# An adaLN megakernel: feed-forward's inner units in single PSUM banks, and empty places between the variance and its root's use

## The chip, the cores and the metric

The kernel runs on one core of a Trainium2 chip, as one launch. The metric is the time on the device in microseconds (us). A core has five queues of instructions that run side by side and wait for each other by semaphores: TensorE (PE, matrix products, with its weight loads shown as PEld), VectorE (DVE), ScalarE (ACT, functions by table), GpSimd (POOL) and SyncE (SP, which starts the DMAs). Matrix products land in PSUM, eight banks of 128 partitions by 512 numbers[...].

## The reference, cut to what matters

The input is 2 sequences of 2048 tokens with 128 features. There are two blocks, each of this form, where the six vectors of each block come from a small modulation:

```
h = layernorm(x) * (1 + ca) + sa ;  x = x + ga * attention(h)
h = layernorm(x) * (1 + cb) + sb ;  x = x + gb * ffn(h)
```

In the first block the attention is a chunked delta-rule form, and its "ffn" is a whole local transformer of six layers with 16 heads and a window of 32. In the second block the attention is a linear-attention layer with its own two layer norms and a Gelu feed-forward, and its "ffn" is a local transformer of two layers with 8 heads and a window of 64. A layer of a local transformer is

```
x = x + local_attention(shift(x) @ Wqkv) @ Wo     # l2-normed, scaled, rotary q and k; softmax
t = shift(x);  v = mean((t - mean(t))**2)
n = (t - mean(t)) / sqrt(v + 1e-5) * g + b
a, gate = split(n @ W1 + b1)                      # 341 units each
x = x + (a * gelu(gate)) @ W2 + b2
```

The norm thus goes variance, root, use of the root. Everything is computed in float32.

## The kernel before, in words

After the first attention (up to about 570 us of the profile) the function `local_models` does the rest: eight layers, six with 16 heads and two with 8. Each layer is 32 tiles of 128 tokens (16 of each sequence, the sequences in turn), 256 tiles in all, and one loop at its end runs over them. In round `i` of that loop the tiles are at different stages: scores of tile i+1, projection of tile i+3 (`project`, L871 to L904), output of tile i.

*A round on PE, in order:* scores (`ps_s`, L986 masks and L995), the first projection (`ps_qk`, L871), the transposes of the softmax's weights (`ps_pT`, L1030), the second projection (only with 16 heads), weights times values (`ps_o`, L1047), values of tile i+2 (`ps_v`, L955), transposes of the output (`ps_oT`, L1063) and of q and k (`ps_turn`, L936), the output projection (`ps_y`, L1075).

*What DVE does in a round:* maximum and shift of the scores (L1003, L1005), two rotary products `r` and `t` for each projection (L881, L886), the row sums of the weights (L1019), the sums of squares (L897), a fast inverse root in eight small instructions that ends in `rq_y` (L167 to L180), and the residual `hs` (L1081). POOL adds r and t (L892), multiplies by the root (L904) and normalises the weights (L1021). ACT squares (L873), takes Exp (L1012) and copies nearly all that leaves PSUM.

*PSUM:* two pairs of banks (`wide`, pool `f_psA`) and four single banks (`bank`, pool `f_psT`). Scores and projections take the pairs in turn. A pair that held a projection comes free when `rq_y` is done, since the root's scratch lies in it.

*Feed-forward.* When four tiles of a sequence are done, `feed_forward` puts six steps for the 512 tokens on a list, and a round takes two places of the list, one after its first projection and one before `project_out`. The steps: `centre` (PE L1103, squares on ACT L1105), `variance` (DVE L1112 and L1115, and the power -0.5 on POOL, L1117), `scale` (PE turns the root into rows, `ps_r` L1135; DVE multiplies, L1138), `gate` and `up` (each through `hidden`, three matmuls L1156; Gelu on ACT L1166, product on DVE L1173) and `down` (PE L1181, sums on DVE L1187). Two sequences give two such blocks in eight tiles.

*Linear attention of the second block.* It works on 512 tokens at a time too. Its 27 steps (the tuple returned by `linear`) are on a second list, of which a round takes six places. They begin when the sixth layer's feed-forward of these tokens is done, and run beside the tiles of the sixth and the seventh layer, about 3520 to 4440 us of the profile. The steps hold three norms: before a3 and f3 `variance` also scales the centred rows on POOL (`xc`, L1120) and the next step turns them on PE (`normed`, `ps_n` L1128); before d4 the root itself is turned (L1135). A place with `rest` is a step that does nothing. A loop at the head of layer seven would take steps until the tokens it needs are ready.

*What sets the order.* The text of the loop gives each engine's order to a list scheduler of the framework, which may move an instruction ahead of others in its engine's queue, and it names the banks when it does so. So the order of the built program has to be looked at, not only the text.

The lines of the loop that take the steps:

```
lstep()                                    # before scores, before and after the rest of project ...
step()                                     # after the first projection
...
step()                                     # after the turns, before project_out
```

Of the kernel before, what the change touches and what calls it, by code (L numbers as in the profile page):

```python
# [24 lines left out]
HSZ = (128, 128, 85)  # L25
# [47 lines left out]
def tile_kernel(ctx: ExitStack, tc: tile.TileContext, a: dict, out: bass.AP):  # L73
# [27 lines left out]
    def bc(ap, shape):  # L101
        return ap.to_broadcast(list(shape))
# [605 lines left out]
    def local_models(mA, mB, hs0):  # L708
# [3 lines left out]
        wk = ctx2.enter_context(tc.tile_pool(name="f_k", bufs=1))  # L712
        lw = ctx2.enter_context(tc.tile_pool(name="l_w", bufs=1))
# [3 lines left out]
        def wide(name):  # L717

            return psA.tile([128, 1024], F32, tag="A", name=f"ps_{name}")

        def bank(name):
            return psT.tile([128, 512], F32, tag="T", name=f"ps_{name}")
# [366 lines left out]
        def step():  # L1089
            if steps:  # L1090
                steps.pop(0)()

        def lstep():
            if lsteps:
                lsteps.pop(0)()
# [3 lines left out]
        def centre(S, x, pool, keep):  # L1099
            p = bank("c")  # L1100
            for j in range(4):
                js = slice(j * 128, (j + 1) * 128)
                nc.tensor.matmul(p[:, js], lhsT=x[:, js], rhs=cen, start=True, stop=True)  # L1103
            S["sq"] = pool.tile([128, 512], F32, name="fsq")
            nc.scalar.activation(S["sq"], p, AF.Square)  # L1105
            if keep:
                S["xc"] = pool.tile([128, 512], F32, tag="t1", name="xc")
                nc.scalar.copy(S["xc"], p)

        def variance(S, pool):  # L1110
            ve = pool.tile([128, 4], F32, name="fve")
            nc.vector.tensor_reduce(  # L1112
                ve, S.pop("sq").rearrange("p (j d) -> p j d", j=4), AX.X, ALU.add
            )
            nc.vector.tensor_scalar(ve, ve, 1.0 / 128.0, 1e-5, ALU.mult, ALU.add)  # L1115
            rt = S["rt"] = pool.tile([128, 4], F32, name="frt")
            nc.gpsimd.tensor_tensor(rt, ve, bc(nhalf, (128, 4)), ALU.pow)  # L1117
            if "xc" in S:
                v = S["xc"].rearrange("p (j d) -> p j d", j=4)
                nc.gpsimd.tensor_tensor(v, v, bc(rt.unsqueeze(2), (128, 4, 128)), ALU.mult)  # L1120
# [10 lines left out]
        def scaled(S, x, out):  # L1131
            p = bank("r")
            rt = S.pop("rt")
            for j in range(4):
                nc.tensor.transpose(  # L1135
                    p[:, j * 128:(j + 1) * 128], bc(rt[:, j:j + 1], (128, 128)), ident
                )
            nc.vector.tensor_tensor(out, x, p, ALU.mult)  # L1138


        def feed_forward(g, b, blk):
            m, l = layers[g]
            n0 = blk * 512
            x = hs[1][:, b, n0:n0 + 512]
            S = {}

            def scale():
                S["x"] = wk.tile([128, 512], F32, tag="fsq", name="fx")
                scaled(S, x, S["x"])

            def hidden(base):
                pw = wide("f")
                ps_ = [pw[:, 0:512], pw[:, 512:1024], bank("f")]
                for c, sz in enumerate(HSZ):
                    o = base + 128 * c
                    nc.tensor.matmul(  # L1156
                        ps_[c][0:sz], lhsT=wts[g, "w1"][:, o:o + sz], rhs=S["x"],
                        start=True, stop=True,
                    )
                return ps_  # L1160

            def gate():
                for c, p in enumerate(hidden(HID)):
                    sz = HSZ[c]
                    u = S[c] = wk.tile([128, 512], F32, name=f"u{c}")
                    nc.scalar.activation(  # L1166
                        u[0:sz], p[0:sz], AF.Gelu, bias=wts[g, "c"][0:sz, 3 + c:4 + c]
                    )

            def up():  # L1170
                for c, p in enumerate(hidden(0)):
                    sz = HSZ[c]
                    nc.vector.scalar_tensor_tensor(  # L1173
                        S[c][0:sz], p[0:sz], wts[g, "c"][0:sz, c:c + 1], S[c][0:sz],
                        ALU.add, ALU.mult,
                    )

            def down():
                p = bank("fy")
                for c, sz in enumerate(HSZ):  # L1180
                    nc.tensor.matmul(  # L1181
                        p, lhsT=wts[g, "w2"][0:sz, c, :], rhs=S[c][0:sz],
                        start=(c == 0), stop=(c == 2),
                    )
                for lo, sh in ((0, 0), (64, 1)):
                    cs = slice(n0 + sh, n0 + sh + 512)
                    nc.vector.scalar_tensor_tensor(  # L1187
                        hs[0][lo:lo + 64, b, cs], p[lo:lo + 64, :], m.vec[lo:lo + 64, l, 8:9],
                        hs[1][lo:lo + 64, b, cs], ALU.add, ALU.add,
                    )  # L1190
                if l == m.depth - 1:
                    lsteps.extend((linear if m is models[0] else output)(b, blk))

            steps.extend((
                lambda: centre(S, x, wk, False), lambda: variance(S, wk), scale, gate, up, down,
            ))

        def outer(b, k, gate, x):
# [55 lines left out]
        def linear(b, k):  # L1254
            S = {}
# [8 lines left out]
            def a0():  # L1264
                outer(b, k, mA, S["x"])

            def rest():
                pass

            def a3():  # L1270
                p = normed(S)
# [139 lines left out]
            def f3():  # L1411
# [8 lines left out]
                ready.add((b, k))  # L1420

            return (
                fetch, rest, a0, lambda: centre(S, S["x"], lw, True), lambda: variance(S, lw), a3,
                rest, lambda: centre(S, S["h"], lw, False), b2, b3, b4, rest, c1, c2, c3, c4, d1,
                rest, lambda: centre(S, S["x1"], lw, False), lambda: variance(S, lw), d4, e1, e2,
                rest, lambda: centre(S, S.pop("x"), lw, True), lambda: variance(S, lw), f3,
            )


# [37 lines left out]
        for i in range(-3, n):  # L1467
            j = i + 3
            lstep()
            if 0 <= i + 1 < n:  # L1470
                scores(i + 1)
# [3 lines left out]
            if j < n:  # L1475
                g, b, t = tiles[j]
                jj = j % per
                nu = len(layers[g][0].units)
                more = g < last
                if g == second and t % 4 == 0:  # L1480
                    while (b, t // 4) not in ready:
                        lstep()
                if nu == 2:
                    project(j, 0)
                if more and jj == 4:
                    load_proj(g + 1, 0)
                if more and jj == 6 and g + 1 == second:
                    models[1].consts()
                if jj == 6 and g == second - 1:
                    linear_consts()  # L1490
                if more and jj == 8:
                    factors(g + 1)
                    if 2 == 2:
                        load_out(g + 1)
                if more and jj == 18:
                    load_ff(g + 1)
                if more and jj == 22:
                    fold_ff(g + 1)
                if nu == 2 and more and jj == per - 1:
                    load_proj(g + 1, 1)  # L1500
                lstep()
# [27 lines left out]
            if i >= 0:  # L1529
                g, b, t = tiles[i]  # L1530
                project_out(i)
                if 2 == 1 and i % per == per - 1 and g < last:
                    load_out(g + 1)
                if t % 4 == 3:
                    feed_forward(g, b, t // 4)
# [9 lines left out]
    with ExitStack() as ctx2:  # L1545
        local_models(m0, m1, hs0)
# [63 lines left out]
```

## Time and profile before

Three runs took 5069.89, 5073.97 and 5086.58 us.

| | |
|---|---|
| median of the runs | 5073.97 us |
| the profiled execution's own time | 5073.89 us |
| its span, first to last instruction | 5072.1 us |
| mean granted PE clock | 0.959 |
| PE busy | 4591.6 us, 91% |
| DVE busy | 3984.3 us, 79% |
| ACT busy | 2861.4 us, 56% |
| POOL busy | 2781.8 us, 55% |
| HBM traffic | 10 GB/s |

The span lies within 1.8 us of the profiled execution's time. The busy time of an engine counts its own instructions, not the time in which its queue stood at a semaphore; the list of waits gives the latter, by the instruction that waited and by what released it. A line like "PE ps_qk L871 <- DVE rq_y L180: 52.6, 51, 3.1" says that the matmul at line 871 waited 51 times for the instruction at line 180, 52.6 us in all and 3.1 at the longest.

### The profile page before, as it was taken

The page shows a single profiled execution, that of the slowest core. Times are in us where ns is not written, and L with a number is a line of the kernel's source. Part 1 is how long each engine was busy: PE and PEld are TensorE (multiplying, and loading weights), DVE is VectorE, ACT ScalarE, POOL GpSimd, SP SyncE. Part 2 cuts the span into 40 slices and gives each one's busy share as a digit, 9 for nine tenths or more (in the row PEclk, how much of TensorE's full clock was granted, in tenths as well). Part 3 has the DMA queues.
Part 4 walks back from the last instruction along what each step waited for, and adds up shares of the span by engine and source line. Part 5 has one row for each costly group of instructions (what it writes and reads, how often), then busy time and mean ns, then how long its engine had stood idle before and what let it go on. Part 6 is the DMA issues. An engine that isn't in the chain of part 4 may idle for free.

```text
span 5072.1 us, 170859 instructions
## 1 busy us (share of the span) xinstructions
PE 4591.6 (91%) x74850; PEld 3154.3 (62%) x74850; DVE 3984.3 (79%) x6840; ACT 2861.4 (56%) x4645; POOL 2781.8 (55%) x1666
## 2 busy tenths in 40 slices
PE   5667799999999999999999999999989898899887
PEld 4445566666666666666666666666666565566554
DVE  6993488888887888788888888888776776688886
ACT  3323356666666666566666666666555554565554
POOL 3332366666665666566666666666555443355553
PEclk8777899999999999999999999999999999999999
DMA  2000222223222322222222222232122211111111
GB/s 76 1 1 24 83 70 63 63 72 79 63 66 63 81 67 71 60 76 69 63 67 66 77 70 67 63 78 68 48 54 52 53 45 40 36 45 43 54 52 41
DMA packets 222489, 295.61 MB, mean 58 GB/s; under 512 B 75656, under 2 KB 95408, under 8 KB 221744
## 3 DMA queue, kind: packets, MB, share of 16 engines
q1 hardware_dynamic: 221744, 284.67, 21.6%
q8 instruction: 591, 9.68, 0.8%
q14 instruction: 154, 1.26, 0.1%
HBM read 40.98 MB, written 10.75 MB: 10 GB/s over the span
## 4 chain that ended last, share of the span: by engine, by line
PE 52%; DVE 21%; ACT 7%; POOL 6%; issue 3%; DMA 1%; POOLq 0%; DVEq 0%; SPq 0%; ACTq 0%
PE ps_qk L871 12%; PE ps_turn L936 5%; PE ps_y L1075 5%; PE ps_v L955 5%; PE ps_o L1047 4%; PE ps_f L1156 4%; DVE t L886 4%; DVE ps_qk L897 4%; POOL r L892 4%; PE ps_s L995 4%; PE ps_fy L1181 3%; PE ps_oT L1063 3%; ACT sq L873 3%; DVE r L881 3%; DVE rs L1019 2%
## 5 line engine op out<-in xcount | busy, mean ns | idle before, releaser
L892 POOL TENSOR_TENSOR r<-r,t 128x1024 f32<-128x1024 f32 x448 | 1061.0, 2368 | 1034.1 <-DVE t L886 940.8
L873 ACT ACTIVATE sq<-ps_qk 128x1024 f32<-128x1024 f32 x448 | 460.1, 1027 | 1093.2 <-PE ps_qk L871 1085.9
L904 POOL TENSOR_TENSOR r<-r,rq_y 128x1024 f32<-128x1024 f32 x448 | 845.8, 1906 | 418.6 <-DVE rq_y L180 416.3
L871 PE MATMUL ps_qk<-wp,hs 128*128 128x512 f32 x1792 | 891.1, 620 | 88.2 <-DVE rq_y L180 63.6
L886 DVE TENSOR_TENSOR t<-ps_qk,tb 128x1024 f32<-128x1024 f32 (+1 forms) x512 | 553.2, 1080 | 173.3 <-POOL r L892 173.3
L1021 POOL TENSOR_TENSOR sm<-sm,rs 128x1024 f32<-128x1024 f32 x256 | 488.3, 1908 | 291.1 <-DVE rs L1020 207.3
L881 DVE TENSOR_TENSOR r<-ps_qk,tb 128x1024 f32<-128x1024 f32 (+1 forms) x512 | 548.7, 1072 | 113.2 <-ACT sq L873 108.7
L897 DVE TENSOR_REDUCE ps_qk<-sq 128x16 f32<-128x1024 f32 x448 | 548.5, 1224 | 10.7
L1047 PEld LDWEIGHTS ps_o<-v,pT 64*32 64x32 f32 (+1 forms) x26624 | 357.9, 108 | 281.9 <-ACT pT L1031 158.3
L871 PEld LDWEIGHTS ps_qk<-wp,hs 128*128 128x128 f32 x1792 | 308.3, 192 | 351.1 <-issue 236.6
L1047 PE MATMUL ps_o<-v,pT 64*32 64x64 f32 (+1 forms) x26624 | 422.9, 223 | 58.5 <-ACT pT L1031 32.4
L1075 PEld LDWEIGHTS ps_y<-oT,wo 128*128 128x128 f32 x3584 | 432.3, 193 | 62.7 <-issue 55.2
L955 PE MATMUL ps_v<-wp,hs 128*128 128x512 f32 x896 | 461.7, 631 | 1.0 <-issue 1.0
L936 PE MATMUL ps_turn<-ident,r 128*128 128x128 f32 x3584 | 448.3, 278 | 7.3 <-POOL r L904 5.8
L1075 PE MATMUL ps_y<-oT,wo 128*128 128x128 f32 x3584 | 447.1, 277 | 1.9 <-ACT oT L1064 1.9
L936 PEld LDWEIGHTS ps_turn<-ident,r 128*128 128x128 f32 x3584 | 411.5, 144 | 13.4 <-POOL r L904 10.6
L1003 DVE TENSOR_REDUCE mx<-ps_s 128x16 f32<-128x1024 f32 (+1 forms) x256 | 313.1, 1223 | 122.4 <-PE ps_s L995 118.9
L1156 PE MATMUL ps_f<-fx,w 128*128 128x512 f32 (+1 forms) x768 | 370.4, 606 | 6.1 <-DVE z L1290 3.5
L995 PE MATMUL ps_s<-kT,qT 64*32 64x64 f32 (+1 forms) x26624 | 366.5, 229 | 0.6 <-issue 0.6
L995 PEld LDWEIGHTS ps_s<-kT,qT 64*32 64x32 f32 (+1 forms) x26624 | 317.3, 107 | 62.1 <-issue 46.1
L1031 ACT COPY pT<-ps_pT 128x512 f32<-128x512 f32 x512 | 273.8, 585 | 143.3 <-PE ps_pT L1030 143.0
L1019 DVE TENSOR_REDUCE rs<-sm 128x16 f32<-128x1024 f32 (+1 forms) x256 | 310.0, 1211 | 53.9 <-ACT sm L1012 53.2
(267 smaller groups left out, 7555.9 us busy)
## 6 DMA issues: line engine op xcount, KB each, us to landing
v<-vn SPq DMA_DIRECT2D x1276, 128.0 KB
v<-vn SPq DMA_DIRECT2D x744, 64.0 KB
v<-vn SPq DMA_DIRECT2D x64, 256.0 KB
wp<-in_L_ffn_Wqkv SPq DMA_DIRECT2D x20, 512.0 KB
xD<-xb SPq DMA_DIRECT2D x24, 256.0 KB
xb<-xD SPq DMA_DIRECT2D x24, 256.0 KB
cs<-in_cos SPq DMA_DIRECT2D x128, 32.0 KB
cs<-in_sin SPq DMA_DIRECT2D x128, 32.0 KB
```

What stands on the lines that cost most here:

```text
L871: nc.tensor.matmul(pq[:, js], lhsT=hw, rhs=wts[g, u][:, js], start=True, stop=True)
L873: nc.scalar.activation(sq, pq, AF.Square)
L881: nc.vector.tensor_tensor(r[:, es].rearrange("p (h d) -> p h d", d=DH), pq[:, es].rearrange("p (h d) -> p h d", d=DH), bc(tb[:, 0, s].unsq ...
L886: nc.vector.tensor_tensor(t2[:, es].rearrange("p (h s d) -> p h s d", s=2, d=32), pq[:, es].rearrange("p (h s d) -> p h s d", s=2, d=32)[: ...
L892: nc.gpsimd.tensor_tensor(r, r, t2, ALU.add)
L897: nc.vector.tensor_reduce(pq[:, 16 * v:16 * v + 16], st[i].pop(("sq", v)).rearrange("p (h d) -> p h d", d=DH), AX.X, ALU.add,)
L904: nc.gpsimd.tensor_tensor(rv, rv, bc(y[:, 16 * v:16 * v + 16].unsqueeze(2), (128, 16, DH)), ALU.mult)
L936: nc.tensor.transpose(p[:, c * 128:(c + 1) * 128], r[:, cs], ident)
L955: nc.tensor.matmul(p, lhsT=hw, rhs=wv, start=True, stop=True)
L995: nc.tensor.matmul(sp[W * w:W * w + W, c0:c0 + 2 * W], lhsT=qT[64 * q:64 * q + 64, cc, W * w:W * w + W], rhs=kT[64 * q:64 * q + 64, cc, W ...
L1047: nc.tensor.matmul(po[s][W * w:W * w + W, co:co + 64], lhsT=pT[kp, q, c, W * w:W * w + W], rhs=v2[kp, w, co:co + 64], start=True, stop=True,)
L1075: nc.tensor.matmul(py[:, 0:128], lhsT=wts[g, "o"][:, c * NO + s, :], rhs=oT[:, s, c, :], start=(c + s == 0), stop=(c == 3 and s == NO - 1),)
```

## The change

Three edits. `hidden`, which serves gate and up, takes three single banks in place of a pair and one single bank. `rest`, the empty step, is defined for all. And an empty step is put between `variance` and the step that uses its result: once in the feed-forward's list (six steps become seven), and three times in the linear attention's (27 become 30). Line numbers after the first edit shift by three, and by two from `hidden` on.

```diff
+        def rest():
+            pass
+
@@
             def hidden(base):
-                pw = wide("f")
-                ps_ = [pw[:, 0:512], pw[:, 512:1024], bank("f")]
+                ps_ = [bank("f") for _ in HSZ]
                 for c, sz in enumerate(HSZ):
@@
             steps.extend((
-                lambda: centre(S, x, wk, False), lambda: variance(S, wk), scale, gate, up, down,
+                lambda: centre(S, x, wk, False), lambda: variance(S, wk), rest, scale, gate, up,
+                down,
             ))
@@
-                fetch, rest, a0, lambda: centre(S, S["x"], lw, True), lambda: variance(S, lw), a3,
+                fetch, rest, a0, lambda: centre(S, S["x"], lw, True), lambda: variance(S, lw), rest,
+                a3,
                 rest, lambda: centre(S, S["h"], lw, False), b2, b3, b4, rest, c1, c2, c3, c4, d1,
-                rest, lambda: centre(S, S["x1"], lw, False), lambda: variance(S, lw), d4, e1, e2,
-                rest, lambda: centre(S, S.pop("x"), lw, True), lambda: variance(S, lw), f3,
+                rest, lambda: centre(S, S["x1"], lw, False), lambda: variance(S, lw), rest,
+                d4, e1, e2,
+                rest, lambda: centre(S, S.pop("x"), lw, True), lambda: variance(S, lw), rest,
+                f3,
```

More of the change, by code (lines that the diff above doesn't have):

```diff
@@ L1265, in a0 @@
                 outer(b, k, mA, S["x"])
-            def rest():
-                pass
             def a3():
```

## The prediction

> **What bounds the kernel now.** I read the page first: TensorE (PE) is busy 91% of the span, and most of the chain that ended last is PE.
>
> ```profile
> PE 4591.6 (91%) x74850; PEld 3154.3 (62%) x74850; DVE 3984.3 (79%) x6840; ACT 2861.4 (56%) x4645; POOL 2781.8 (55%) x1666
> ...
> PE 52%; DVE 21%; ACT 7%; POOL 6%; issue 3%; DMA 1%; POOLq 0%; DVEq 0%; SPq 0%; ACTq 0%
> ```
>
> Next, the busy times tile by tile, cut where `project_out` (L1075) starts, for eight tiles of the six 16-head layers. Columns: start and end, length, busy time of each engine.
>
> ```profile
> 1852.54:1868.00 15.46, 15.28 (x328) 11.42 (x327) 13.65 (x23) 10.20 (x19) 11.74 (x8) 1.00 0.31 77
> 1868.00:1886.51 18.51, 17.43 (x330) 12.03 (x329) 16.72 (x27) 12.30 (x21) 13.05 (x8) 1.00 0.33 82
> 1886.51:1907.47 20.96, 19.93 (x331) 12.67 (x330) 16.39 (x32) 13.34 (x21) 12.22 (x9) 1.00 0.20 52
> 1907.47:1922.50 15.03, 15.03 (x327) 11.30 (x326) 11.57 (x14) 8.53 (x15) 7.44 (x5) 1.00 0.21 50
> 1922.50:1941.13 18.63, 17.46 (x331) 12.05 (x330) 16.84 (x27) 12.31 (x21) 13.95 (x9) 1.00 0.35 88
> 1941.13:1961.32 20.19, 19.70 (x331) 12.57 (x330) 16.39 (x32) 13.24 (x21) 11.46 (x8) 1.00 0.18 45
> 1961.32:1975.73 14.41, 14.36 (x320) 10.33 (x318) 10.90 (x13) 7.94 (x14) 7.59 (x4) 1.00 0.25 59
> 1975.73:1990.74 15.01, 14.37 (x321) 10.31 (x320) 13.16 (x22) 9.77 (x18) 10.45 (x7) 1.00 0.29 74
> sum 138.20, PE 133.58 PEld 92.69 DVE 115.61 ACT 87.61 POOL 87.91; mean PE 16.70 PEld 11.59 DVE 14.45 ACT 10.95 POOL 10.99
> ```
>
> Rows 1 to 3 carry one feed-forward block (centre and variance; scale and gate; up and down), rows 4 to 6 another, rows 7 and 8 none. PE is idle 138.20-133.58 = 4.6 us in eight tiles: all that any reordering can win here, 20 such groups giving 92 us. What ends PE's waits, by stage (first the 16-head layers, 900 to 3500 us; then 3520 to 4440, where the linear attention of the second block runs beside the tiles; then the last 630 us):
>
> ```profile
> PE ps_qk L871 <- DVE rq_y L180: 52.6, 51, 3.1
> PE ps_o L1047 <- ACT pT L1031: 18.0, 38, 0.5
> ```
> ```profile
> PE ps_n L1128 <- POOL xc L1120: 47.3, 14, 7.2
> PE ps_r L1135 <- POOL frt L1117: 18.6, 5, 5.1
> ```
> ```profile
> PE ps_oT L1063 <- ACT on L1053: 16.3, 25, 0.9
> PE ps_o L1047 <- ACT pT L1031: 10.2, 29, 1.2
> ...
> PE ps_r L1135 <- POOL frt L1117: 6.8, 4, 4.3
> ```
>
> The middle pair is PE standing behind the root and the scaling on POOL in the linear attention's norms: 66 us. In the feed-forward of the 16-head layers the same root waits for PE, not PE for it, as the timeline shows (root at 1506, used at 1512.6):
>
> ```profile
> 1506.08 1.03 POOL L1117 TENSOR_TENSOR frt<-fve,nhalf 128x4 f32<-128x4 f32 x1
> ...
> 1512.63 0.60 PE L1135 MATMUL ps_r<-ident,frt 128*128 128x128 f32 x4
> ```
>
> ScalarE's table switches, one to Gelu and one back to Exp for nearly each of 64 feed-forward blocks:
>
> ```profile
> L1012 ACT ACT_TABLE_LOAD x68 | 87.2, 1283 | 19.0 <-DVE sm L1005 17.9
> L1166 ACT ACT_TABLE_LOAD x62 | 79.5, 1283 | 0.5
> ```
>
> **What the Trainium skill says.** "TensorE: Matmul & The Clock Gate" (section Architectural detail) has matmuls in order with only weight loads pulled ahead, and ACT and DVE strictly first in, first out: the waits above, with everything behind them late, agree. "PSUM — Partial Sum Buffer" (PSUM bank collisions) wants PSUM guarded by bank, so a bank is free only when its last reader is done; here that makes qk wait for rq_y, 52.6 us. "Perfetto Trace Analysis" (Optimization Strategy) reads a gap that repeats on the saturated engine as perhaps too few PSUM buffers; the repeating 0.5 us behind pT and 1 us behind rq_y fit. "ScalarE: Activation LUTs" (What ACT_TABLE_LOAD costs) prices a switch at 1283 ns and a drain of 1380 ns; the trace agrees on 1283, and shows no drain (load at 1523.35, Gelu at 1524.64).
>
> **The change, part by part.** No arithmetic, DMA or operand is added or removed; SP's queue keeps its entries. Three things move; the built order of both programs shows how.
>
> *Single banks.* Gate and up no longer take two of the four banks that scores and qk alternate in; they take three of the other four. The wait this removes, qk behind a Gelu, is not in the list of waits: worth 0 by itself. New waits: behind up, the second pT, v and o now stand on the u products (DVE). Beside L1075-to-L1047 work of 7 us these products, the first ahead of r0, are done 1 to 2 us before: 0.
>
> *The empty place in the feed-forward.* Two places per tile, six steps become seven, so the two blocks of a group now fall differently. The order of a group becomes: root transposes; gate and up; down and centre; nothing; root and gate; up and down; nothing; centre. Removed: the split up (one of its matmuls among the pT transposes), with 18.0/18.6 groups = 0.97 us of pT waits per group (900 to 3500 us holds 18.6 groups of 139.7 us). Left: one tile where three Gelus and a table load stand on ACT between Exp and the pT copies. Worked from durations: qk starts at 0, ends 1.95; scores' shift on DVE done 3.1, Exp (1.06) 4.15, load 5.45, three Gelus (about 0.65) 7.5, pT copy 8.1; PE has by then done gate (2.6), pT, the second qk and two mask matmuls, 7.7: waits 0.45. Saved 0.5.
> The qk wait: in a light tile DVE's loop is about 15.0 us against 14.4 of PE (rows 7, 8); the variance adds 0.87 to DVE, the root's product 0.68, a centre 0.6 to PE (15.03-14.41), root transposes 0.44. Before, four waits per group: after rows 7, 8, 1 (0.4, 0.6, 0.8), and after the lone row 4, where down's sums and the variance meet, 1.2: 3.0 (list: 52.6/18.6 = 2.8). After: 0.4, 0.65, and 0.8 behind the tile that holds only the root; the lone light tile has its variance before `hs1`, where DVE waits for PE anyway: 0.1. Sum 1.95, saved 1.0. Together 1.5 us a group, 20 groups: **-30 us**. If the light tiles behave worse than this arithmetic, 0; at most three quarters of 92, -70.
>
> *The empty places in the linear attention.* 27 steps become 30, six places a tile, so each block ends half a tile later (last ready at tile 210 for 205; wanted at 214): no forced draining, cost 0. PE work counted between the centring matmuls and the use, with the durations above: 16 transposes of the scaled rows 3.4 us before, 6.4 after; the eight d4 roots 3.4 and 6.0. Chain now: 3.4 + 47.3/16 = 6.4 us (single ones 3.5 to 10); against the new cover some 20 us of waits remain, saved 27. Roots: 3.4 + 18.6/8 = 5.7, remain 8, saved 11. PE is busy 87% here (174.76 of 200 us, 3900 to 4100) and DVE 69% (138.94), so most is kept; three quarters of 38: **-29 us** (-10 to -50).
>
> *The last two layers (8 heads).* DVE and PE are closer here (89.4 and 93.3 of 104.4 us in eight tiles at 4823). The built program has 158 table loads for 138: 8 more in the last layer, 13 more in the one before (one less earlier). There Exp falls between the second and third Gelu: load, Exp, load, third Gelu, two pT copies. PE is through gate, pT and qk at 7.8 us after the scores' start, the first copy ends at 10.3: a stall of about 2.5, seven times, +18; the short root waits (6.8-4.3 at the very end) go, -3. **+15 us** (0 to +35). The end itself is unchanged, the empty step costing nothing there.
>
> Sum: -30 - 29 + 15 = -44 on the profiled execution, 5073.9 us (span 5072.1 and 1.8 around it), which equals the median shown, 5073.97: 5030.
>
> **Rivals.**
> *Only the linear attention gains* (16-head layers unmoved because DVE's loop, not the order, sets the light tiles): -29+15, about 5058. For it: the 52.6 us behind rq_y are DVE's. Against: DVE is busy 115.6 of 138 us, so placing matters.
> *Waits reappear behind DVE in the linear stage*: with PE going on, DVE there keeps 10 us of the 29: about 5050; joined with the first, 5080.
> *All placing works*: -60, -45, 0: about 4970. For it: the ceilings of 92 and 66 us.
> *Slower: ACT in gate-first tiles.* One tile in eight, some 30 in all, has the table load and three Gelus ahead of the pT copies and the second square. I gave 0.45 us to each of 23 in the 16-head layers. If Exp is late there, PE stands longer; from 2.4 us (23 x 1.9 = 44) it decides, at 3.5 the kernel takes 5030+70 = 5100. For it: the 18 us that already stand on pT. Against: DVE's shift is early in those tiles.
> *The change does nothing to the order* is excluded: the built orders differ.
>
> **How the numbers follow.** My forecast (5005 to 5058) 0.50; linear only or reappearing waits (5045 to 5085) 0.23; all works 0.12; slower 0.15. Likeliest 5031. Range 4985 to 5085. Within 0.3% (5059 to 5089) is about what a measurement cannot tell from no change: faster 0.73, same 0.13, slower 0.14.
>
> **What would show it.** In the profile after: `ps_n` behind POOL down from 47 to near 20 and `ps_r` in the linear stage to under 10; qk behind rq_y near 35 in 900 to 3500; pT waits about 9 there; eight tiles 136.7 us; more table loads by 20; the last layer some 10 us longer. Wrong if eight tiles are no shorter, if `ps_o` behind pT grows beyond 18, or if a new wait of PE behind u or hs0 (DVE) appears.

## The result, and the profile after

The changed kernel takes 4995.36 us (median of five runs, 4988.67 to 5005.95) against 5077.64 us for the kernel before on the same chip (5069.89 to 5086.58): a ratio of 0.9839, 95% interval 0.9817 to 0.9861. It is faster, and by more than the forecast, which was 5031 us. Its profiled execution took 5004.3 us with a span of 5002.5, against a span of 5072.1 before: 69.6 us less. The page of the kernel after, engines and chain:

```profile
PE 4572.7 (91%) x74820; PEld 3143.2 (63%) x74850; DVE 3973.1 (79%) x6840; ACT 2883.5 (58%) x4665; POOL 2780.8 (56%) x1666
...
PE 53%; DVE 20%; ACT 8%; POOL 5%; issue 3%; DMA 1%; SPq 0%; POOLq 0%; ACTq 0%; DVEq 0%
```

The page hardly moves. The stages do. Cutting both traces where `project_out` starts for a tile gives the length of each stretch of tiles:

| tiles | what runs there | before | after | difference |
|---|---|---|---|---|
| 0 to 168 | 16-head layers alone | 2929.8 | 2890.6 | -39.2 |
| 168 to 212 | linear attention beside the sixth and seventh layer | 941.4 | 879.3 | -62.1 |
| 212 to 255 | the 8-head layers alone | 526.2 | 558.2 | +32.0 |

These sum to -69.3, so nearly the whole difference is in the table. The same eight tiles of the 16-head layers as in the prediction (columns: start and end, length, busy time of PE, PEld, DVE, ACT, POOL), three rows and the sum:

```profile
1851.49:1870.35 18.86, 15.31 (x325) 11.06 (x323) 16.88 (x29) 10.20 (x18) 13.77 (x9) 1.00 0.25 62
...
1890.81:1908.03 17.22, 17.22 (x331) 12.22 (x330) 14.87 (x20) 10.32 (x16) 10.56 (x7) 1.00 0.23 57
1908.03:1922.44 14.41, 14.41 (x320) 10.33 (x319) 12.35 (x19) 9.13 (x17) 8.90 (x6) 1.00 0.28 68
...
sum 137.38, PE 133.35 PEld 92.69 DVE 114.19 ACT 87.09 POOL 85.97; mean PE 16.67 PEld 11.59 DVE 14.27 ACT 10.89 POOL 10.75
```

The sum was 138.20. Work has moved between the rows: the fourth (from 1890.81) holds down and a centre now, and the lone light tile behind it takes 14.41 us, for 15.03. PE is idle in neither; over the eight tiles it is idle 4.0 us, for 4.6, and 3.55 of the 4.0 now stand in the second tile (18.86 - 15.31). Over all of tiles 32 to 160, a group of eight takes 2210.8/16 = 138.2 us, against 139.7. What ends PE's waits in the 16-head layers (880 to 3480 us), then from tile 168 to 212 (3526.9 to 4406.2), then in the last 630 us:

```profile
PE ps_qk L871 <- DVE rq_y L180: 31.4, 40, 3.1
PE ps_o L1047 <- issue: 22.1, 16, 2.3
PE ps_o L1047 <- ACT pT L1031: 5.6, 19, 0.6
```
```profile
PE ps_n L1131 <- POOL xc L1123: 9.0, 5, 3.8
...
PE ps_c L1106 <- DVE ps_qk L167: 7.0, 4, 2.3
...
PE ps_r L1138 <- POOL frt L1120: 6.4, 4, 2.4
```
```profile
PE ps_oT L1063 <- ACT on L1053: 23.4, 39, 0.8
PE ps_o L1047 <- ACT pT L1031: 19.0, 27, 2.5
```

A wait put down to "issue" is one for nothing that the profile shows; at `ps_o` these were 12.0 us before. Behind the root and the scaling PE now stands 15.4 us in the linear stage, for 65.9 before. In the last layers the waits behind ACT have grown from 16.3 and 10.2 to 23.4 and 19.0. The feed-forward's root, finished long before PE wanted it, now waits still longer (1498.4 to 1514.2):

```profile
1497.40 1.02 POOL L1120 TENSOR_TENSOR frt<-fve,nhalf 128x4 f32<-128x4 f32 x1
...
1514.21 0.60 PE L1138 MATMUL ps_r<-ident,frt 128*128 128x128 f32 x4
```

The table loads of Exp and of the feed-forward's Gelu, 68 and 62 before:

```profile
L1012 ACT ACT_TABLE_LOAD x76 | 97.5, 1283 | 49.9 <-DVE sm L1005 48.7
L1168 ACT ACT_TABLE_LOAD x68 | 87.2, 1283 | 1.2
```

### The profile page after: what moved, and what is told of

It reads as the page before. It is cut to its first block, busy times and chain, and to the rows that moved or that the text cites. A ratio compares the mean times of both kernels' runs of the same rounds, so it can differ in the third digit from the quotient of the medians.

```text
span 5002.5 us, 170719 instructions
## 1 busy us (share of the span) xinstructions
PE 4572.7 (91%) x74820; PEld 3143.2 (63%) x74850; DVE 3973.1 (79%) x6840; ACT 2883.5 (58%) x4665; POOL 2780.8 (56%) x1666
## 4 chain that ended last, share of the span: by engine, by line
PE 53%; DVE 20%; ACT 8%; POOL 5%; issue 3%; DMA 1%; SPq 0%; POOLq 0%; ACTq 0%; DVEq 0%
PE ps_qk L871 11%; PE ps_v L955 6%; PE ps_f L1158 5%; PE ps_turn L936 5%; PE ps_y L1075 5%; PE ps_o L1047 5%; PE ps_s L995 4%; DVE ps_qk L897 4%; POOL r L892 3%; DVE t L886 3%; PE ps_fy L1183 3%; PE ps_oT L1063 3%; ACT sq L873 2%; DVE r L881 2%; PE ps_pT L1030 2%
## 5 line engine op out<-in xcount | busy, mean ns | idle before, releaser
L897 DVE TENSOR_REDUCE ps_qk<-sq 128x16 f32<-128x1024 f32 x448 | 549.1, 1226 | 12.3
L955 PE MATMUL ps_v<-wp,hs 128*128 128x512 f32 x896 | 471.9, 639 | 1.0 <-ACT on L1053 0.6
L1158 PE MATMUL ps_f<-fx,w 128*128 128x512 f32 (+1 forms) x768 | 356.4, 600 | 1.7 <-DVE fx L1141 1.7
L956 ACT COPY vn<-ps_v 128x512 f32<-128x512 f32 x448 | 262.5, 586 | 112.3 <-PE ps_v L955 93.4
```

Of the source, the lines that this page charges most:

```text
L897: nc.vector.tensor_reduce(pq[:, 16 * v:16 * v + 16], st[i].pop(("sq", v)).rearrange("p (h d) -> p h d", d=DH), AX.X, ALU.add,)
L955: nc.tensor.matmul(p, lhsT=hw, rhs=wv, start=True, stop=True)
L1158: nc.tensor.matmul(ps_[c][0:sz], lhsT=wts[g, "w1"][:, o:o + sz], rhs=S["x"], start=True, stop=True,)
```

## The experiments

All times are medians, each with its ratio to the kernel before on the same chip. The three right-hand columns are lengths in the profile, as differences from the profile of before (2929.8, 941.4 and 526.2 us). Each kernel has one profile. Where kernels have the same code in a stretch, the first column differs by up to 12 us between them (the 16-head layers of the change, e4, e5, e6 and e8), the last by up to 5 (the 8-head layers of before, e3, e5, e7 and e9 to e12). e4's profile is the slowest of its four runs, 4992.8 us. The runs were made on several chips, on which the median of the kernel before was 5070.1 to 5077.6 us. The start of tile 0 itself varies by some 13 us between profiles (631.8 to 645.3 us), so the stretches tell parts apart more finely than the totals do.

| kernel | us | ratio, 95% interval | 0 to 168 | 168 to 212 | 212 to 255 |
|---|---|---|---|---|---|
| the change | 4995.4 | 0.9839 [0.9817, 0.9861] | -39 | -62 | +32 |
| e1, banks alone | 5042.8 | 0.9933 [0.9919, 0.9947] | -33 | +3 | +7 |
| e2, feed-forward's place alone | 5107.1 | 1.0058 [1.0043, 1.0074] | 0 | +21 | +13 |
| e3, linear attention's places alone | 5063.3 | 0.9978 [0.9969, 0.9987] | 0 | -4 | -3 |
| e4, change, no place with 8 heads | 4973.3 | 0.9804 [0.9784, 0.9824] | -29 | -64 | +11 |
| e5, change, 8 heads as before | 4976.4 | 0.9791 [0.9775, 0.9807] | -35 | -65 | -3 |
| e6, change, pair with 8 heads | 4977.0 | 0.9806 [0.9792, 0.9819] | -41 | -66 | +11 |
| e7, e3 and three places ahead | 4997.7 | 0.9849 [0.9836, 0.9861] | -4 | -70 | -4 |
| e8, change and three places ahead | 5060.2 | 0.9968 [0.9956, 0.9979] | -37 | -14 | +34 |
| e9, no feed-forward place, three ahead | 4964.3 | 0.9789 [0.9769, 0.9810] | -33 | -70 | -3 |
| e10, e7 with late centres | 5009.7 | 0.9876 [0.9856, 0.9896] | +3 | -60 | -3 |
| e11, e9 with two ahead | 4977.6 | 0.9812 [0.9791, 0.9832] | -33 | -62 | -4 |
| e12, e9 with four ahead | 4962.2 | 0.9769 [0.9747, 0.9791] | -28 | -81 | -4 |

### The three parts, each alone

The first theory was that of the prediction: the feed-forward's place gains in the 16-head layers, the linear attention's places gain in their own stage, the banks nothing. The rival: the banks make the first gain.

e1 takes only this edit:

```diff
-                pw = wide("f")
-                ps_ = [pw[:, 0:512], pw[:, 512:1024], bank("f")]
+                ps_ = [bank("f") for _ in HSZ]
```

> Only the single banks for gate and up; no empty place is added. My theory: the wait that the banks remove (a projection behind a Gelu) was never in the list of waits, so nothing is won by them: within 10 us of the kernel before, 5065 to 5085, the eight-tile group of the 16-head layers as long as before (139.7 us), ps_n behind POOL still about 47 us. Rival (the gain of the 16-head layers comes from scores and projections having the pairs to themselves): 5035 to 5050, the group near 138.2 us. The table loads stay at 138 in both.

e2 takes only this one:

```diff
-                lambda: centre(S, x, wk, False), lambda: variance(S, wk), scale, gate, up, down,
+                lambda: centre(S, x, wk, False), lambda: variance(S, wk), rest, scale, gate, up,
+                down,
```

> Only the empty place in the feed-forward's list; gate and up keep the pair and the linear attention's 27 steps. My theory: the new placing of the steps is what shortens the 16-head layers (-37 us over layers one to five and a little in the sixth) and what lengthens the 8-head layers (table loads split around Exp, 154 loads; +17 in the last layer and up to +15 in the one before): sum between -20 and 0, 5055 to 5077, the group of eight near 138.3 us, last layer near 13.0 us a tile. Rival (the banks make the 16-head gain): the group stays at 139.7 and the kernel is slower than before by 15 to 35 us.

e3 takes only the linear attention's 30 steps in place of its 27 (the last hunk of the change).

> Only the three empty places in the linear attention; feed-forward as before. My theory: PE's waits behind the root and the scaling on POOL (66 us) fall to about 15, and all of that reaches the end: -45 to -60, 5018 to 5033; the 16-head group at 139.7 and the last layer at 12.5 us a tile as before. Rival (the stage is held by DVE and ACT as well, as I discounted in the prediction, and a good part of the 51 us that tiles 168 to 192 won comes from the feed-forward's placing): -20 to -35, 5043 to 5058.

e4 is the whole change, but the feed-forward's empty place stands in the 16-head layers only:

```diff
-                lambda: centre(S, x, wk, False), lambda: variance(S, wk), rest, scale, gate, up,
+                lambda: centre(S, x, wk, False), lambda: variance(S, wk),
+                *((rest,) if m is models[0] else ()), scale, gate, up,
```

> All of the change, but the empty place in the feed-forward's list only in the 16-head layers; the 8-head layers have six steps as before, with single banks. My theory: the loss of the last layer (+17 us) and of the pure part of the seventh layer (about +8) comes from the empty place there, which lets Exp fall between the second and third Gelu; without it the last layer has 16 table loads and about 12.5 us a tile, and the kernel takes 20 to 28 us less than the changed one: about 4972. Rival (the loss comes from the single banks, where up's products hold banks that pT, o and v want): the last layer stays near 13.0 us a tile and the kernel near 4995.

*In the 16-head layers the banks do it.* e1 has -33 of the -39 us, e2 none. The other kernels agree: with single banks alone these layers take 2896.3 to 2902.3 us (e1, e9, e11, e12), with the place as well 2888.6 to 2900.9 (the change, e4, e5, e6, e8), with neither 2926.0 to 2933.1 (before, e3, e7, e10). In e1 the waits of `ps_o` behind pT are gone from the list, while qk still waits 50.2 us for rq_y (900 to 3500 us, 52.6 before). In e2 the waits behind rq_y do fall as the prediction said, but a new wait takes the gain away, and that behind pT halves only. PE's waits in e2, 900 to 3500 us:

```profile
PE ps_qk L871 <- DVE rq_y L180: 31.3, 45, 3.1
PE ps_o L1047 <- issue: 21.3, 20, 2.2
PE ps_qk L871 <- DVE t L886: 17.9, 19, 1.2
PE ps_o L1047 <- ACT pT L1031: 8.7, 18, 0.5
```

52.6 - 31.3 = 21.3 us saved, 17.9 spent again in the tile that now holds gate and up together: the pair they take there is one that qk wants. The 9.3 us less behind pT are offset by the waits put down to "issue", 21.3 for 12.0. In the tile of up in the kernel before, the second projection, which in the other tiles stands between the transposes of pT and `ps_o` and covers the copies, is pushed into the middle of `ps_o`. With single banks it stands in front again. Before, and then e1:

```profile
1896.07 0.39 PE L1047 MATMUL ps_o<-v,pT 64*32 64x64 f32 x10 [0.48 <-ACT pT L1031]
1896.39 1.98 PE L871 MATMUL ps_qk<-wp,hs 128*128 128x512 f32 x4
1898.30 1.43 PE L1047 MATMUL ps_o<-v,pT 64*32 64x64 f32 x117
```
```profile
1879.62 1.88 PE L871 MATMUL ps_qk<-wp,hs 128*128 128x512 f32 x4
1881.43 1.57 PE L1047 MATMUL ps_o<-v,pT 64*32 64x64 f32 x128
```

That fits the vanished wait; no run isolates it further. Nor is it all of e1's gain: in tiles 32 to 160 PE is idle 15.3 us less than before and busy 8.1 us less (2158.4 and 2150.3) for the same 41730 recorded matmuls, and why it is less busy stays open. In the whole change PE waits 16.3 us less behind rq_y than in e1 there (25.3 and 41.6), and the tiles take only 1.7 us less, since 4.4 come back behind pT, 5.8 under "issue" and 4.0 as busy time. A list of waits that gets shorter isn't yet a gain.

*In the linear stage the parts don't add up.* Banks +3, feed-forward's place +21, linear attention's places -4, together -62. e3 itself, at 5063.3 us, missed the range of the theory and that of its rival. Something must come about only when the parts are joined. e4 kept the -64 and lost most of the loss behind tile 212, which put it below the changed kernel.

### Where in the round the linear attention's steps fall

The steps hold four norms, one more than the description of the kernel says; the root of the second is used by DVE (in b3) and got no empty place. A round takes six of the steps. Thirty steps are exactly five rounds, so that every block falls on the same places of the rounds. Which ones is decided when the first block is put on the list, by `down` of the sixth layer. Without the feed-forward's empty place, `down` is in the second of a round's two places, with it in the first of the next: three steps of the linear attention later. So the new theory: the gain hangs on the phase, which the feed-forward's place happens to shift. e7 is e3 with that shift and nothing else; e8 shifts the whole change by the same three, which puts it where e3 was.

```diff
                 if l == m.depth - 1:
+                    if m is models[0] and b == 0 and blk == 0:
+                        lsteps.extend([rest] * 3)
                     lsteps.extend((linear if m is models[0] else output)(b, blk))
```

> The linear attention's three empty places alone, and three further empty places once, ahead of its very first block, so that its 30 steps start at the phase that the whole change gives them; pair and six feed-forward steps as before. Theory of the phase: tiles 168 to 212 fall from 937 to 875-890 us and the time from 5063 to 5003-5015. Rival (the linear stage needs the single banks or the feed-forward's later root for its gain): 925 to 940 us there, 5055 to 5066 in all.

> The whole change, and the same three empty places once ahead of the first linear block, which puts its steps at the phase that they have with the linear attention's empty places alone. Theory of the phase: tiles 168 to 212 rise from 879 to 920-940 us and the time from 4995 to 5035-5055. Rival: 875 to 890 us, 4990 to 5003 in all.

The theory holds in both directions. e7 falls from 5063.3 to 4997.7 us, a little more than expected, and as fast as the whole change; its stage takes 871.2 us. e8 rises from 4995.4 to 5060.2 (some 5 us above the range given), its stage to 927.9.

What the bad phase looks like is plain in e3's trace, where tiles 171, 176, 181 and 186, every fifth, take 34.6 to 38.4 us (in e7 the longest takes 29.9). In one of them PE stands for the linear attention's output `at`. Its input was there at 3904.98, but DVE did two sums of squares of the round (L897, 1.23 and 1.21 us) and a copy (1.32) before it, and `at` was done at 3909.36. PE's timeline in e3, and then the granted clock in two stretches of 5 us and in the one that stands at half (the last three columns are PEclk, DMA share, GB/s):

```profile
3909.51 1.08 PE L1370 MATMUL ps_aT<-ident,at 128*128 128x128 f32 x4 [4.35 <-DVE ps_qk L167]
3910.39 3.24 PE L955 MATMUL ps_v<-wp,hs 128*128 128x512 f32 x4
```
```profile
3905.00:3910.00 5.00, 0.65 (x22) 0.52 (x5) 5.00 (x13) 1.07 (x2) 3.18 (x3) 0.63 0.15 36
3910.00:3915.00 5.00, 5.00 (x16) 2.69 (x15) 1.66 (x8) 1.76 (x3) 3.50 (x2) 0.69 0.14 32
3906.28:3913.11 6.83, 3.60 (x8) 2.08 (x9) 4.91 (x17) 1.17 (x2) 3.72 (x4) 0.50 0.13 31
```

The wait is put down to L167, which ran at the same moment; what the transposes read is `at`, L1362. Half of the clock is granted from 3906.28 to 3913.11, that is from 1.1 us after PE began to stand to 3.6 us after it went on, and four matmuls take 3.24 us that take 1.98 at full clock (the projection at 3899.63). Here the wait is paid for a second time in the work behind it, with some 1.8 us, half of the 3.60 us that PE is busy in this stretch (an estimate). "TensorE: Matmul & The Clock Gate" (Why this matters for your kernels) advises against idle gaps of PE above some 3 us for this reason; the 4.35 us here agree. But three waits of 2.15, 1.60 and 1.49 us, with 0.50 and 0.42 us of work between them, were followed by half of the clock as well (3885.80 to 3892.63 us of the same trace), so here shorter waits that lie close had the same sequel.

The norms tell the same. In e3, from the variance (L1115, L1118) over root (L1120) and scaled rows (L1123) to their transposes, in lines of DVE, POOL and PE:

```profile
3953.04 0.63 DVE L1115 TENSOR_REDUCE fve<-fsq 128x4 f32<-128x512 f32 x1
3953.58 2.46 DVE L1205 SCALAR_TENSOR_TENSOR xb<-hs,L_m,xb 64x512 f32<-64x512 f32 x1
...
3957.10 1.20 DVE L886 TENSOR_TENSOR t<-ps_qk,tb 128x1024 f32<-128x1024 f32 x1
3958.23 0.15 DVE L1118 TENSOR_SCALAR fve<-fve 128x4 f32<-128x4 f32 x1
3958.45 2.34 POOL L892 TENSOR_TENSOR r<-r,t 128x1024 f32<-128x1024 f32 x1 [2.95 <-DVE fve L1118]
3960.74 1.47 POOL L1120 TENSOR_TENSOR frt<-fve,nhalf 128x4 f32<-128x4 f32 x1
...
3963.69 1.12 PE L1131 MATMUL ps_n<-ident,xc 128*128 128x128 f32 x4 [5.57 <-POOL xc L1123]
```

And one in e7:

```profile
3726.44 0.69 DVE L1115 TENSOR_REDUCE fve<-fsq 128x4 f32<-128x512 f32 x1 [1.70 <-ACT fsq L1108]
3727.16 1.52 DVE L1118 TENSOR_SCALAR fve<-fve 128x4 f32<-128x4 f32 x1
3728.76 1.02 POOL L1120 TENSOR_TENSOR frt<-fve,nhalf 128x4 f32<-128x4 f32 x1
...
3733.63 0.60 PE L1131 MATMUL ps_n<-ident,xc 128*128 128x128 f32 x4
```

In e3 the small second half of the variance stands behind a product of the next block (L1205) and the rotary products on DVE, and the root behind the addition of r and t on POOL: 10.65 us from L1115 to the transposes (3963.69 - 3953.04), 5.57 of them bare. In e7 nothing stands between, the rows are ready at 3730.89, and PE takes them at 3733.63 without a wait. Over tiles 168 to 212, PE's waits behind xc and frt are 65.9 us before, 26.4 in e3 (all behind xc) and 9.2 in e7; those of `ps_aT` behind DVE and of the transposes of z (L1311) are 37.5 us in e3, while in e7 the list has 2.6 for `ps_aT` and none for z.

### Cover or phase

The prediction had put the gain down to more PE work between the centring and the use of the root. e10 takes most of this cover away in the good phase: centre and variance of the three norms fall one place later than in e7, and every other step keeps its place:

```diff
-                fetch, rest, a0, lambda: centre(S, S["x"], lw, True), lambda: variance(S, lw), rest,
+                fetch, rest, a0, rest, lambda: centre(S, S["x"], lw, True), lambda: variance(S, lw),
                 a3,
...
-                rest, lambda: centre(S, S["x1"], lw, False), lambda: variance(S, lw), rest,
+                rest, rest, lambda: centre(S, S["x1"], lw, False), lambda: variance(S, lw),
                 d4, e1, e2,
-                rest, lambda: centre(S, S.pop("x"), lw, True), lambda: variance(S, lw), rest,
+                rest, rest, lambda: centre(S, S.pop("x"), lw, True), lambda: variance(S, lw),
                 f3,
```

> As the linear attention alone with three places ahead of its first block (4997.7 us; tiles 168 to 212 at 871), but each of the three new empty places stands before its centre instead of between variance and the root's use, so that every other step keeps its place. If the cover between centre and use makes the gain: PE's waits for the root and the scaled tensor go from 9 us back to 30 to 50, tiles 168 to 212 to 905 to 930, the time to 5030 to 5055. If the fixed phase alone makes it: at most 885 us there and 5010 in all.

The stage takes 881.3 us and the kernel 5009.7: in this phase the added cover makes a small part of the gain. Moving the three places costs 881.3 - 871.2 = 10 us, about what the waits behind xc and frt grow (16.8 us for 9.2). The other 60 us come with the steps' places. The cover can be counted in the traces, as PE's busy time between the last centring matmul and the transposes of the scaled rows: on average 4.0 us before, 4.7 in e10, 7.0 in e3 and 7.2 in e7. e3, with half as much again as e10, waits longer (26.4 us behind xc for 10.8). No run takes the cover away in the bad phase, so what it is worth there is not shown; nor is it shown apart what the period of exactly five rounds does, which e3, e7 and e10 all have and the 27 steps don't. Cover counted on PE says little while DVE and POOL are not free to do the covered work.

### The 8-head layers

The prediction had given the loss there to the table loads that the empty place brings. e5 gives the 8-head layers back both the pair and the six steps, e6 only the pair:

```diff
-                ps_ = [bank("f") for _ in HSZ]
+                if models[0] is m:
+                    ps_ = [bank("f") for _ in HSZ]
+                else:
+                    pw = wide("f")
+                    ps_ = [pw[:, 0:512], pw[:, 512:1024], bank("f")]
```

> Single banks and the empty place of the feed-forward in the 16-head layers only, linear attention as in the change; the feed-forward of the two 8-head layers is that of the kernel before (the pair, six steps). If the loss in the 8-head layers comes from banks and empty place together: 4958 to 4968 us, last layer 385 to 392 us between tiles 224 and 255 (change 404.3, only the empty place taken out there 396.6). If it comes from the empty place alone: 4970 to 4976, as without the place there. If it is handed down from the linear stage's different end: last layer still 396 or more.

> The whole change, but with the pair of PSUM banks in the 8-head layers; the empty place stays there, and so do the added table loads. If the table loads made the loss (the step of the prediction): last layer 402 or more, time 4990 to 5000. If the loss needs the single banks (the theory now): last layer 387 to 393, time 4975 to 4988, for only the gate tile then waits as with the empty place alone.

With e4 (banks alone there) and the change (both) this is a square. Tiles 212 to 255 take 523.3 us in e5 with neither, 537.4 with the empty place alone (e6), 536.9 with the banks alone (e4), 558.2 with both: +14.2, +13.7 and +34.9. Each costs, and together they cost some 7 us more than their sum. Of the place's 14.2 us, about 5 are moved work: twelve more matmul records of the seventh layer's feed-forward fall behind tile 212 (an estimate by their durations). The totals of e4, e5 and e6 are not distinguishable (their intervals overlap, and e5's 4976.4 is above the range expected for it), so the square rests on one profile each; e1, e2 and e8 have the same code there as its other three corners, and with +7, +13 and +34 they show the same. What the two do together is in the tile that holds gate and up. ACT and PE after, in the last layer:

```profile
4672.23 1.06 ACT L1012 ACTIVATE sm<-sm 128x1024 f32<-128x1024 f32 x1
4673.30 1.28 ACT L1168 ACT_TABLE_LOAD   x1
...
4675.19 1.05 ACT L1031 COPY pT<-ps_pT 128x512 f32<-128x512 f32 x2
...
4675.81 0.33 PE L1047 MATMUL ps_o<-v,pT 128*64 128x64 f32 x4 [2.53 <-ACT pT L1031]
```

The Exp stands between the second and third Gelu, the pT copies wait behind load and third Gelu, and PE stands 2.53 us: the mechanism and the size of one stall that the prediction gave. In e6 the same ACT order leaves 4.5 us of waits behind pT in the whole last layer (14.7 after), because the pair holds back up's matmuls, and PE has them to do in that time; it waits 6.5 us for the pair there instead. The tile takes 15.7 us in e6 and 18.8 to 20.2 after. The wait is only part of that. This tile after and in e6, and the stretch behind the wait:

```profile
4665.40:4685.62 20.22, 17.01 (x115) 10.47 (x114) 12.62 (x26) 13.29 (x19) 9.34 (x6) 0.83 0.13 38
4676.82:4683.65 6.83, 6.14 (x43) 4.87 (x43) 3.71 (x5) 3.62 (x7) 2.37 (x2) 0.50 0.28 77
```
```profile
4652.63:4668.30 15.67, 14.05 (x112) 8.11 (x111) 11.12 (x24) 12.28 (x18) 8.07 (x6) 1.00 0.16 43
```

Of the 4.55 us between them, 1.6 are idle time and 3.0 busy time: behind the wait PE works for 6.83 us at half of the clock. The same wait of 2.5 us stands in all five such tiles behind tile 212 (216, 224, 232, 240, 248), and behind each of them the clock is at half for 3.4 or 6.8 us. It does not follow every wait of this length: in tile 236 of the kernel before and of e7 PE stands 2.6 us, and the clock of the tile is 0.86 there and 1.00 here.

### The feed-forward's empty place, and other phases

If the feed-forward's place does nothing but shift the phase, it can be left out altogether. e9 is e5 without it, with three empty places ahead of the first linear block:

```diff
-                *((rest,) if m is models[0] else ()), scale, gate, up, down,
+                scale, gate, up, down,
```

> No empty place in any feed-forward: single banks in the 16-head layers, the pair in the 8-head ones, the linear attention's three empty places, and three more once ahead of its first block. If the feed-forward's empty place does nothing in the whole change but shift the linear attention's phase: tiles 32 to 160 at 2210 to 2216 us, 168 to 212 at 868 to 882, 224 to 255 at 381 to 388, and 4955 to 4972 us in all. If it has a gain of its own (the step of the prediction, 1.5 us per group of eight tiles): tiles 32 to 160 at 2222 or more, and 4980 or more.

It comes out as the theory says, 4964.3 us, with 2209.6 us for tiles 32 to 160 (2210.8 in the change, 2212.5 in e1) and 871.2 for 168 to 212. e11 and e12 have two and four places ahead in place of three:

> The kernel without an empty place in the feed-forward, two places ahead of the first linear block instead of three. If the good phase is broad: tiles 168 to 212 within 15 us of the three-place kernel, 4955 to 4985 us. If it is one lucky place: 895 or more there and 4990 or more in all.

> The same with four places ahead of the first linear block. If the good phase is broad: tiles 168 to 212 within 15 us of the three-place kernel, 4955 to 4985 us. If it is one lucky place: 895 or more there and 4990 or more in all.

The stage takes 879.9, 871.2 and 860.8 us with two, three and four places: the good phase is broad. e12, at 4962.2 us and 0.9769 of the kernel before, is the fastest measured; its interval lies below that of the changed kernel. e9 and e12 are not told apart by their totals. One and five places were not tried.

## Why the prediction was right or wrong

The sign was right, the time within the range, the forecast 36 us too high; each of its four steps put a gain or a loss in the wrong place or left a part of it out. That the sum came so near is in part luck: the steps missed by -9, -33 and +17 us and the signs differ; the rest is that the profiled execution lies 9 us above the median.

**Single banks, "worth 0 by itself".** Wrong. They are worth -33 us in the 16-head layers (e1). The step looked for the removed wait, qk behind a Gelu, in the list, and did not find it. It missed that a pair held by the feed-forward changes where the second projection stands, and that the pT waits of 18.0 us came from there. It also took PE's idle time as all that an order can win, and of e1's gain in tiles 32 to 160 a third is busy time (8.1 of 23.4 us). The banks cost 13.7 us in the 8-head layers too (e4 against e5), which had no term of its own.

**Feed-forward's place, -30 us.** The stage has -39, the waits it named moved as it said (behind rq_y 31.4 us, forecast 35; behind pT 5.6, forecast 9; eight tiles 138.2 on average, from 139.7, so 1.5 us a group), and still the step was wrong: it gave to the empty place what the banks do. Alone the place gives nothing (e2), since waits of qk behind t and under "issue" take back what is saved behind rq_y and pT; e9 has the gain without it. The rival "only the linear attention gains" falls too: these layers did gain, through the banks.

**Linear attention, -29 us.** Here -62 was measured. The term had three faults. Waits behind xc and frt fell by 50.5 us, not 38; some 7 of that came back in other waits, such as `ps_c` behind DVE (7.0). The discount of a quarter left out of account that PE's busy time also falls: over tiles 168 to 212 from 833.2 to 814.2 us for practically the same matmuls (10584 and 10578 recorded), while the granted clock rose from 0.95 to 0.97. So of the 62 us, 43 are idle time and 19 busy time; the clock accounts for about as much (5% of 941 us less 3% of 879, some 21 us, an estimate). And the cause was wrong: the same edit alone yields 4 us (e3), since the phase decides; in the good phase the added cover is worth 10 (e10 against e7). That the phase would come out well was luck in the prediction, which had taken each part for itself.

**The 8-head layers, +15 us.** The measured +32 is about twice that. The stall of 2.5 us is real, though it comes five times behind tile 212 and not seven, and the idle time grows by 14.6 us, as estimated. Tiles 212 to 255 before and after (length, PE busy, and so on, the clock third from the end):

```profile
4507.54:5033.73 526.19, 479.40 (x4565) 312.64 (x4563) 447.17 (x913) 308.87 (x482) 278.34 (x174) 0.99 0.18 50
4406.16:4964.35 558.19, 496.78 (x4577) 321.51 (x4576) 442.17 (x919) 327.28 (x497) 278.74 (x175) 0.97 0.17 47
```

The missing term is busy time, 17.4 us more. The clock of 0.97 for 0.99 makes some 11 of it and the moved feed-forward about 5 (both estimates). By edits, the place alone costs 14.2 us (e6), the banks alone 13.7, and both together about 7 more. That e6 agrees with the +15 is chance: in e6 no wait behind pT is above 1.1 us in the last layer.

**The rivals.** "All placing works" (4970) is nearer to 4995 than the forecast, but its shares are not the ones measured: -60, -45 and 0 for -39, -62 and +32. "Slower by ACT in gate-first tiles" did not come about in the 16-head layers (pT waits 5.6 us), and did in the last layer, at four tiles of it, and at one tile ahead of it. "Waits reappear behind DVE" in the linear stage came true for the 7 us named above, and did not decide. Of the signs named as proof against it, a new wait of PE behind `u` or `hs0` is not among the leading waits in the 16-head layers; pT waits there did not exceed 18.

## What to carry to other kernels

When two lists of steps are woven into a loop, the place in the round at which a list begins can be worth as much as any edit (66 us between e3 and e7): shift it by a few empty steps, and measure, before crediting a change that happens to shift it. Price a wait of the engine that bounds the kernel above its own length, and look at the granted clock behind it, as in the gate tiles of the last layer, where the lower clock cost about as much as the wait. Cover is not only work on the waiting engine: ask what stands in front of the covered work in its own queues.

## What the runs showed of the hardware that was not expected

PE's busy time made nearly a third of the linear stage's gain (19 of 62 us), at a granted clock of 0.97 for 0.95. A wait of 4.35 us in e3 went with 6.83 us at half of the clock, in which four wide matmuls took 3.24 us for 1.98. Waits of 2.5 us were enough in the changed kernel: all five in the gate tiles behind tile 212 were followed by half of the clock for 3.4 or 6.8 us. It is not certain at that length: a wait of 2.6 us in tile 236 went with a clock of 0.86 in the kernel before and of 1.00 in e7.
